# Segment attention with batch normalization: the last stage with groups in pairs in another order, two units each on ScalarE, rows by segment, nine buffers

## The chip, the cores and the metric

The kernel runs on one core of a Trainium2 chip. A core has TensorE (PE, matrix products into eight PSUM banks), VectorE (DVE), ScalarE (ACT), GpSimd (POOL, which here starts indirect DMAs) and SyncE (SP, which here starts plain DMAs). Each runs its own list of instructions in order, and they wait for one another by semaphores. The metric is the device time of one execution in microseconds (us).

## The reference

16,384 rows of 256 features carry a segment id from 0 to 7, and the ids are not sorted. A position is the row's index less the start that a binary search over the ids gives for its segment. Rows are put into a table of 8 segments by 3,072 positions (a negative position counts from the end, one beyond the table is dropped); each segment attends over itself, and each row reads its place in the result. A linear layer, a batch normalization over all rows, a ReLU and the residual follow:

```
starts = jnp.searchsorted(bids, jnp.arange(B, dtype=bids.dtype))
pos = jnp.arange(N, dtype=bids.dtype) - starts[bids]
...
scores = jnp.where(mask[:, None, :], scores, NEG)
attn = jax.nn.softmax(scores, axis=-1)
rp = jnp.einsum('blm,bmd->bld', attn, vp)
r = rp[bids, pos]
t = r @ Wt
mu = t.mean(axis=0)
var = t.var(axis=0)
tn = (t - mu) / jnp.sqrt(var + EPS) * gamma + beta
return feat + jax.nn.relu(tn)
```

## The kernel before

Only few rows have a place of their own in the table: at most six tiles of 128 rows per segment. All others read one of 16 edge rows (the first and last position of each segment). So there are two kinds of output.

**Segments (`for e in range(NB)`, lines 1581 to 1669).** For each segment the rows are gathered into `xs`, transposed, projected (`project`, `values`), and scored; `attend(e, u)` makes tile `u` on PE, and `attended(e, u)` takes DVE's reciprocal `rdens` and ACT's scaled copy into `tk`. Tiles 4 and 5 are present in some segments only (`present`, a branch on a register). `square` (ACT) and `moments` (DVE) add each tile and its square to `acc`, weighted by how many rows read it (`reads_r`). After tiles 3 and 5 `tk` is also stored to `t_rows` in HBM, from which POOL gathers the edge rows (`ecat`) and rows that are read twice (`tl`). In the last segment tiles 4 and 5 go through `attended` whether they are present or not, and the squares and sums of `tl` lie between its tiles.

**Sums (1671 to 1713).** PE adds the last segment's edge rows (`sel` by `tk`, into `b_e`), then the sums (`ones` by `acc`, `we` by `ecat`). DVE makes of these scale and shift (`ss`), and then the normalized edge rows in three bf16 parts, `y3`.

**Last stage (1723 to 1769).** The 16,384 output rows are 16 groups of 128 by 8 rows of 256, 1 MB each. Eight buffers `fb` hold groups: `group_in` loads one on SP. A group has four units of 2 rows (one PSUM bank each). A unit's one-hot matmuls (`hot`, 48 partitions, from partition 0 for groups 0 to 7 and from 64 for 8 to 15) pick the edge rows; three units are added to the loaded rows by DVE, one (`by_act`) gets the loaded rows through an identity matmul and is copied back by ACT. Then SP stores the group. After each group DVE normalizes three of the 48 tiles of `tk` (`normal`, three steps); the tiles of `tl` come after group 11.

These tiles must overwrite what the groups store, so POOL's row stores (`put`) of segment `e` wait until as many groups have landed as `upto[e]` says. SP counts these in `done` (`finish`), one group behind the store. The stores of `tl` wait for all 16:

```
1762        pg.op("POOL", lambda x, e=e: (x.wait_ge(done, 1), x.wait_ge(done, pg.regs[("POOL", ("g", e))])), [], [])
1767    pg.op("POOL", lambda x: x.wait_ge(done, NG), [], [])
```

**What sets the order.** A recorder (`Program.op`) notes every operation with the memory that it reads and writes, and derives the waits. Each engine executes its operations in the order of the text, so where a line stands in `fast_path` is where it stands in its engine's list. SP's list goes ahead of the others where it has nothing to wait for. `slot` puts pieces of table work into the segments' loop. At the end comes a check for inputs that this path can't handle (`bad`), and after a barrier a branch past the general path.

## Time and profile before

| | |
|---|---|
| median of three runs | 385.09 us (384.39 to 388.5) |
| profiled execution | 389.27 us, span of its records 387.2 us |
| busy in the span | PE 271.6, DVE 249.5, ACT 126.5, POOL 122.4 us |
| granted TensorE clock, mean | 0.795 |
| HBM traffic | 26.79 MB read, 28.74 MB written |
| last stage, from `y3` to the last row store | 273.9 to 370.8 us |

The helpers record all operations, so a line of the profile is a helper's line: L799 is a matmul, L818 a tensor-tensor operation, L809 an activation, L814 a copy on ACT, L874 a gather, L884 a row store, L869 a DMA on SP, L1750 a group's store, L1727 the count of `finish`. Operations are told apart by their tiles. `[0.84 <-DMA tl]` is idle time ahead of an operation and what ended it.

### The profile page before, as it was taken

To read this page: it belongs to the slowest core of one execution; us is meant where nothing else is said; L and a number is where in the kernel's file an instruction comes from. 1 tells how busy PE (TensorE), PEld (TensorE's weight loads), DVE (VectorE), ACT (ScalarE), POOL (GpSimd) and SP (SyncE) were. 2 spreads that over 40 slices of the span, in tenths; PEclk is the share of its full clock that TensorE was granted. 3 is DMA by queue.
4 is the path that set the end of the run, shared out by engine and by line. 5 is a ranking of instruction groups with operands and counts; after the bars stand their busy time and mean duration, and the time that the engine had idled before them with its cause. 6 is when DMAs were issued, how large, how long until landed. Compare 5 with 4: busy or idle time off the path is not lost.

```text
span 387.2 us, 4300 instructions
## 1 busy us (share of the span) xinstructions
PE 271.6 (70%) x1162; PEld 171.1 (44%) x1162; DVE 249.5 (64%) x728; ACT 126.5 (33%) x269; POOL 122.4 (32%) x120
## 2 busy tenths in 40 slices
PE   1247785892697899999999898854699999640000
PEld 1234463571374677677777685640243322110000
DVE  6674388697886767637638335365899999995000
ACT  0022522442434646835844736642011111010000
POOL 1623024061033015006006007620123377751720
PEclk9997788797888999999999999995555555555555
DMA  8971002121111213202202101259999999995200
GB/s 247 341 209 41 2 14 66 64 62 39 47 47 54 80 50 99 90 29 66 76 22 75 57 29 28 77 194 383 422 307 408 424 422 421 383 389 235 96 21 11
DMA packets 26000, 59.34 MB, mean 153 GB/s; under 512 B 5212, under 2 KB 18607, under 8 KB 21866
## 3 DMA queue, kind: packets, MB, share of 16 engines
q1 hardware_dynamic: 19242, 48.06, 33.1%
q0 software_dynamic: 5088, 10.19, 8.2%
q10 hardware_dynamic: 1632, 0.66, 0.6%
q8 instruction: 15, 0.25, 0.3%
q14 instruction: 23, 0.19, 0.2%
HBM read 26.79 MB, written 28.74 MB: 143 GB/s over the span
## 4 chain that ended last, share of the span: by engine, by line
PE 41%; DVE 26%; issue 10%; ACT 8%; DMA 6%; POOL 3%; SPq 1%; POOLq 0%; ACTq 0%; DVEq 0%
PE ps L799 39%; DMA out<-f 4%; DVE acc L838 3%; DVE f L818 3%; POOL out L884 3%; DVE tk L818 3%; ACT pb L809 2%; ACT tk L809 2%; DVE w L818 2%; DVE junk L825 2%; DVE k L815 2%; ACT pa L809 2%; PE ps L804 1%; DMA graw<-in_L_rec_beta 1%; ACT vs L814 1%
## 5 line engine op out<-in xcount | busy, mean ns | idle before, releaser
L874 POOL DMA_INDIRECT xs<-in_r_feat,idx x48 | 53.9, 1124 | 157.1 <-DVE idx L838 46.4
L799 PE MATMUL ps<-vs,pa 128*128 128x257 f32 x312 | 75.0, 388 | 1.8 <-ACT vs L814 1.8
L799 PEld LDWEIGHTS ps<-vs,pa 128*128 128x128 f32 x312 | 58.1, 192 | 15.4 <-issue 4.7
L884 POOL DMA_INDIRECT out<-tk,idx x39 | 44.0, 1128 | 40.0 <-SPq L1727 29.0
L809 ACT ACTIVATE tk<-ps,rdens 128x256 f32<-128x256 f32 x48 | 23.0, 479 | 79.1 <-DVE rdens L851 79.1
L799 PE MATMUL ps<-wvt,xT 128*128 128x256 f32 x156 | 43.1, 428 | 7.6 <-ACT vs L814 6.0
L799 PE MATMUL ps<-y,hot 48*128 48x256 bf16 x128 | 33.5, 409 | 12.8 <-DVE y L815 7.5
L799 PEld LDWEIGHTS ps<-wvt,xT 128*128 128x128 f32 x156 | 32.6, 215 | 20.9 <-ACT vs L814 7.7
L799 PEld LDWEIGHTS ps<-y,hot 48*128 48x128 bf16 x128 | 12.2, 123 | 51.6 <-issue 24.1
L799 PE MATMUL ps<-f,ident 128*128 128x512 f32 x32 | 33.2, 1140 | 0.0
L799 PE MATMUL ps<-q,k 32*128 32x512 f32 (+2 forms) x154 | 20.0, 530 | 16.0 <-ACT tk L809 16.0
L814 ACT COPY f<-ps 128x512 f32<-128x512 f32 x16 | 9.4, 585 | 66.6 <-PE ps L799 66.6
L818 DVE TENSOR_TENSOR tk<-tk,ss 128x768 f32<-128x768 f32 x32 | 30.5, 953 | 0.5
L818 DVE TENSOR_TENSOR f<-f,ps 128x512 f32<-128x512 f32 x48 | 30.0, 679 | 0.8 <-PE ps L799 0.8
L809 ACT ACTIVATE pa<-ps,mask 128x512 f32<-128x512 f32 x39 | 23.8, 687 | 18.2 <-PE ps L799 18.1
L838 DVE SCALAR_TENSOR_TENSOR acc<-tk,reads_r,acc 128x256 f32<-128x256 f32 x48 | 23.0, 479 | 10.5 <-ACT tk L809 10.3
L815 DVE COPY k<-ps 32x128 f32<-32x128 f32 x40 | 11.8, 294 | 24.2 <-PE ps L799 23.8
L838 DVE SCALAR_TENSOR_TENSOR acc<-sq,reads_r,acc 128x256 f32<-128x256 f32 x48 | 23.1, 481 | 1.8 <-ACT sq L809 1.8
L851 DVE RECIPROCAL rdens<-ps 128x1 f32<-128x1 f32 x48 | 7.8, 162 | 23.7 <-PE ps L799 23.4
L799 PE MATMUL ps<-xT,w 128*128 128x512 f32 (+1 forms) x60 | 22.6, 512 | 0.4 <-ACT xT L809 0.3
L799 PE MATMUL ps<-vs,pb 128*128 128x257 f32 x82 | 19.6, 387 | 0.0
L809 ACT ACTIVATE sq<-tk 128x256 f32<-128x256 f32 x48 | 19.2, 413 | 1.0
(231 smaller groups left out, 338.4 us busy)
## 6 DMA issues: line engine op xcount, KB each, us to landing
f<-in_r_feat SPq DMA_DIRECT2D x16, 1024.0 KB, 9.0
out<-f SPq DMA_DIRECT2D x16, 1024.0 KB, 9.9
xs<-zt SPq DMA_DIRECT2D x8, 768.0 KB, 10.2
t_rows<-tk SPq DMA_DIRECT2D x8, 512.0 KB, 2.9
t_rows<-tk SPq DMA_DIRECT2D x8, 256.0 KB, 2.2
eb<-edge_of SPq DMA_DIRECT2D x16, 96.0 KB, 2.4
xs<-in_r_feat,idx POOLq DMA_INDIRECT x48, 2.8
out<-tk,idx POOLq DMA_INDIRECT x39, 6.5
```

The costliest lines, as they stand in the source:

```text
L799: "PE", lambda e: e.matmul(out, lhsT, rhs, start=start, stop=stop, skip_group_check=True),
L804: return self.op("PE", lambda e: e.transpose(out, in_, ident), [in_, ident], [out])
L809: "ACT", lambda e: e.activation(out, in_, func, bias=bias, scale=scale), [in_, *more], [out]
L814: return self.op("ACT", lambda e: e.copy(out, in_), [in_], [out])
L815: return self.op(eng, lambda e: e.tensor_copy(out, in_), [in_], [out])
L818: return self.op(eng, lambda e: e.tensor_tensor(out, a, b, op), [a, b], [out])
L825: lambda e: e.tensor_scalar(out, a, s1, s2, op0, op1, accum_out=accum)
L838: else e.scalar_tensor_tensor(out, a, s, b, op0, op1),
L851: return self.op("DVE", lambda e: e.reciprocal(out, in_), [in_], [out])
L874: lambda e: e.indirect_dma_start(out=out, out_offset=None, in_=table, in_offset=bass.IndirectOffsetOnAxis(ap=ind, axis=0), bounds_check=n ...
L884: lambda e: e.indirect_dma_start(out=table, out_offset=bass.IndirectOffsetOnAxis(ap=ind, axis=0), in_=src, in_offset=None, bounds_check=n ...
```

## The change

- **Groups in pairs.** Groups are processed in an order of their own (`ORDER`: 0 to 6, 15 down to 12, 7 to 11), two at a time. The first of a pair uses one-hots on partitions 0 to 47, the second on 64 to 111, and their matmuls alternate. Two units of each group (`x >= 4`), not one, go through the identity matmul and ACT.
- **Gates.** `upto[e]` is now the highest turn among the groups that overlap a segment's positions, from both sides (`turn_of`).
- **Rows by segment.** After pair `c` DVE normalizes the rows of segment `c`: tiles 0 to 3 together, 4 and 5 each if present.
- **Buffers.** Nine instead of eight, over memory that is laid out anew. The first three loads are issued during segment 6, the others from segment 7 on as their memory comes free.
- **Sums.** The factor 1/N moves into `ones_n` and `we`. In the last segment the square of a tile is read from PSUM, tiles 4 and 5 are skipped if absent, the sums of tile 3 to 5 are made by PE (`by_reads`), and `tl` is gathered in segment 6, squared at once into `tq` ahead of the last segment's first tile, and added after its second. The edge rows gathered from `t_rows` are added by PE (`ident` by `ecat`).
- **Splitting `y3`** takes one operation less per part; `reads_r` of segment 6 is gathered; the check's DVE work moves to the first pair.

```diff
+    ORDER = (0, 1, 2, 3, 4, 5, 6, 15, 14, 13, 12, 7, 8, 9, 10, 11)
...
+        last = e == NB - 1
+        with present(e, u if last else 0):
+            pg.recip(rdens[:, m : m + 1], po[:, D : D + 1])
+        if last and u >= 4:
+            pg.set("DVE", spot2[:], 0.0)
+        with present(e, u if last else 0):
+            pg.act(tk[:, m, :], po[:, 0:D], AF.Identity, scale=rdens[:, m : m + 1])
+            if last:
+                pg.act(sq[m % 4][:], po[:, 0:D], AF.Square, scale=rdens[:, m : m + 1])
...
+            pg.tt(gcmp[:], gcmp[:], by_g(turn_of[:]), ALU.mult)
+            pg.red(grp[:], gcmp[:], ALU.max)
+            pg.ts(upto[:], grp[:], 1.0, ALU.max)
...
-    def group_in(g, after=()):
-        pg.dma("SP", fb[g][:], feat3[g], after)
+    def group_in(i, after=()):
+        pg.dma("SP", fb[i % NF][:], feat3[ORDER[i]], after)
...
+            if e >= NB - 3 and u == 2:
+                gather_reads(e + 1)
+            if e == NB - 2 and u == 3:
+                for t in range(LT):
+                    pg.gather(
+                        tl[:, t, :], t_rows[0 : (NB - 2) * FW, :], ridl[:, t : t + 1], (NB - 2) * FW
+                    )
+            if e == NB - 2 and u == 1:
+                group_in(0)
+            if e == NB - 2 and u == 4:
+                group_in(1)
+                group_in(2)
...
+    edges = pg.gather(ecat[:, 0, :], t_rows[0 : (NB - 1) * FW, :], eidx[:], (NB - 1) * FW)
+    pg.act(tq[:], tl[:], AF.Square)
+    for u in range(4):
+        attend(e, u)
+        for x in ready:
+            moments(*x)
+        ready = [(e, u)]
+        if u == 1:
+            for t in range(LT):
+                pg.tt(acc[:, 0, :], acc[:, 0, :], tl[:, t, :], ALU.add)
+                pg.tt(acc[:, 1, :], acc[:, 1, :], tq[:, t, :], ALU.add)
+        if u == 2:
+            for t in range(3, FT):
+                m = e * FT + t
+                pg.ts(by_reads[:, t - 3, :], ones_n[:], reads_r[:, m : m + 1], ALU.mult)
+        attended(e, u)
+        if u == 0:
+            group_in(3, [edges])
+        if u == 2:
+            scores(e, 1, None)
+            group_in(4)
+    group_in(5)
+    for u in (4, 5):
+        attend(e, u)
+        mark(ps_o[u % 2])
+        attended(e, u)
+    pg.mm(b_e[:, 0:D], ident[:], ecat[:, 0, :], start=True, stop=False)
+    pg.mm(sums[:], ones_n[:], acc[:].rearrange("p s d -> p (s d)"), start=True, stop=False)
...
+    for u in (4, 5, 3):
+        m = e * FT + u
+        with present(e, u):
+            pg.mm(sums[:, 0:D], by_reads[:, u - 3, :], tk[:, m, :], start=False, stop=False)
+            pg.mm(sums[:, D : 2 * D], by_reads[:, u - 3, :], sq[m % 4][:], start=False, stop=False)
+    for i in range(6, NF):
+        group_in(i)
...
-        pg.ts(yf[:], yh[:], later[:, s : s + 1], ALU.mult)
-        pg.tt(ye[:], ye[:], yf[:], ALU.subtract)
+        pg.stt(ye[:], yh[:], later[:, s : s + 1], ye[:], ALU.mult, ALU.add)
...
+    def rows(e):
+        m = e * FT
+        parts = [
+            ((lambda lo=lo: present(e, lo)), tk[:, m + lo : m + hi, :], xs[:, m + lo : m + hi, :], hi - lo)
+            for lo, hi in ((4, 5), (5, 6), (0, 4))
+        ]
+        normal(parts)
...
+    for c in range(NG // 2):
+        pair = (2 * c, 2 * c + 1)
+        for x in range(0, GT, 2):
+            by_act = x >= 4
+            pf = [bank[x + r] for r in range(2)]
             if by_act:
-                pg.mm(pf[:], ident[:], rows, start=True, stop=False)
+                for r, i in enumerate(pair):
+                    pg.mm(pf[r][:], ident[:], unit(i, x), start=True, stop=False)
             for u in range(2):
+                for r, i in enumerate(pair):
+                    h = slice(64 * r, 64 * r + 6 * NB)
+                    pg.mm(
+                        pf[r][:, u * D : (u + 1) * D], hot[h, c, x + u, :], y3[h, :],
+                        start=not by_act, stop=True,
+                    )
...
+            if i >= 2:
+                finish(stores[i - 2])
+                if i - 2 + NF < NG:
+                    group_in(i - 2 + NF)
+        rows(c)
```

Three places in the engines' lists, each before and after. The first is ACT at the passage from segment 6 to segment 7: `vs_66` are segment 7's values, the first `tk` below them is its tile 0, the names with `sq` are its square buffers, and `of_POOL_18` and the like are landings of gathers. Before:

```order
L814 COPY vs_66<-ps 128x2x256 [waits at_PE]
L809 ACTIVATE tk<-ps,rdens 128x256 [waits at_DVE]
L809 ACTIVATE sq_84<-tk 128x256 [waits at_ACT]
L809 ACTIVATE tk<-ps,rdens 128x256 [waits at_DVE]
L809 ACTIVATE sq_85<-tk 128x256 [waits at_ACT]
```

After:

```order
L814 COPY vs_66<-ps 128x2x256 [waits at_PE]
L809 ACTIVATE tq<-tl 128x768 [waits of_POOL_18,of_POOL_19,of_POOL_20]
L809 ACTIVATE tk<-ps,rdens 128x256 [waits at_DVE]
L809 ACTIVATE sq_72<-ps,rdens 128x256
L809 ACTIVATE tk<-ps,rdens 128x256 [waits at_DVE]
L809 ACTIVATE sq_73<-ps,rdens 128x256
```

The square of `tl` now stands ahead of tile 0, with a wait for three gathers.

The second is PE from the last segment's end to the sums; `ones,ident` is `mark`. Before:

```order
L799 MATMUL ps<-ones,ident 128x1 [waits at_ACT]
L799 MATMUL ps<-tk,sel 128x256 x3
L764 COMPARE_AND_BRANCH
L799 MATMUL ps<-tk,sel 128x256 [waits at_ACT]
L764 UNCONDITIONAL_BRANCH
L764 COMPARE_AND_BRANCH
L799 MATMUL ps<-tk,sel 128x256 [waits at_ACT]
L764 UNCONDITIONAL_BRANCH
L799 MATMUL ps<-tk,sel 128x256
L799 MATMUL ps<-acc,ones 128x512 [waits at_DVE]
L799 MATMUL ps<-ecat,we 128x512 [waits at_ACT]
```

After, up to the last `sel` (the `by_reads` products and `ecat,we` follow):

```order
L799 MATMUL ps<-ones,ident 128x1 [waits at_ACT]
L799 MATMUL ps<-ecat,ident 128x256 [waits of_POOL_21]
L799 MATMUL ps<-acc,ones_n 128x512
L799 MATMUL ps<-tk,sel 128x256 x3
L764 COMPARE_AND_BRANCH
L799 MATMUL ps<-tk,sel 128x256 [waits at_POOL,at_ACT]
L764 UNCONDITIONAL_BRANCH
L764 COMPARE_AND_BRANCH
L799 MATMUL ps<-tk,sel 128x256 [waits at_ACT]
L764 UNCONDITIONAL_BRANCH
L799 MATMUL ps<-tk,sel 128x256
```

The product with `acc` moved ahead of `sel`, `ecat,ident` is new, and so are the two to six products with `by_reads`.

The third is PE in the last stage; `y_99` and `y_102` are `y3`, the names with `f` the buffers. Before, one group:

```order
L799 MATMUL ps<-f_70,ident 128x512 [waits at_ACT,of_SP_14]
L799 MATMUL ps<-y_99,hot 128x256 x2
L799 MATMUL ps<-y_99,hot 128x256 [waits at_DVE]
L799 MATMUL ps<-y_99,hot 128x256
L799 MATMUL ps<-y_99,hot 128x256 [waits at_DVE]
L799 MATMUL ps<-y_99,hot 128x256
L799 MATMUL ps<-y_99,hot 128x256 [waits at_DVE]
L799 MATMUL ps<-y_99,hot 128x256
```

After, one pair:

```order
L799 MATMUL ps<-y_102,hot 128x256 [waits at_DVE] x2
L799 MATMUL ps<-y_102,hot 128x256 x2
L799 MATMUL ps<-y_102,hot 128x256 [waits at_DVE] x2
L799 MATMUL ps<-y_102,hot 128x256 x2
L799 MATMUL ps<-f_78,ident 128x512 [waits at_ACT,of_SP_13]
L799 MATMUL ps<-f_79,ident 128x512 [waits at_ACT,of_SP_15]
L799 MATMUL ps<-y_102,hot 128x256 x4
L799 MATMUL ps<-f_78,ident 128x512 [waits at_ACT]
L799 MATMUL ps<-f_79,ident 128x512 [waits at_ACT]
L799 MATMUL ps<-y_102,hot 128x256 x4
```

A pair has four identity products where two groups had two, and neighbouring one-hot products now belong to different groups.

More of the change, by code (lines that the diff above doesn't have):

```diff
@@ L988, in fast_path @@
     we = new("we", [2 * NB, P])
-    cnt_f = new("cnt_f", [P, NL])
+    cnt_f, turn_of = new("cnt_f", [P, NL]), new("turn_of", [1, NG])
     tmp_at = addr(tk) + (3 * FT - 2) * D * 4
@@ L1083, in fast_path @@
     pg.set("DVE", eps_t[:], EPS)
+    pg.set("DVE", ones_n[:], 1.0 / N)
+    pg.set("DVE", rdens[:], 1.0)
     def zero_fill(e):
@@ L1273, in attended @@
         m = e * FT + u
-        pg.recip(rdens[:, m : m + 1], po[:, D : D + 1])
-        pg.act(tk[:, m, :], po[:, 0:D], AF.Identity, scale=rdens[:, m : m + 1])
+        last = e == NB - 1
[7 more added lines that the diff above has]
+                pg.act(sq[m % 4][:], po[:, 0:D], AF.Square, scale=rdens[:, m : m + 1])
+        if last and u >= 4:
+            pg.copy("ACT", spot[:], ones[:, 0:1])
         if u in (3, 5):
@@ L1566, in fill_rows @@
     def fill_rows():
+        for i, g in enumerate(ORDER):
+            pg.set("POOL", turn_of[:, g : g + 1], float(i + 1))
         pg.set("DVE", xl[:], 0.0)
@@ L1580, in fast_path @@
     work.extend(everyone())
-    for e in range(NB):
+    for e in range(NB - 1):
         n = e + 1
-        if n < NB:
-            for eng in ("PE", "ACT", "DVE"):
-                pg.register(eng, n, tiles_i[0:1, n : n + 1], 2)
+        for eng in ("PE", "ACT", "DVE"):
+            pg.register(eng, n, tiles_i[0:1, n : n + 1], 2)
         if e == 0:
@@ L1613, in fast_path @@
             lag.append((e, u))
-            for _ in range(0 if e == 0 else 2 if u % 2 or e == NB - 1 else 1):
+            for _ in range(0 if e == 0 else 2 if u % 2 else 1):
                 if lag:
@@ L1686, in fast_path @@
-    sums = ps_s[1]
-    pg.mm(sums[:], ones[:], acc[:].rearrange("p s d -> p (s d)"), start=True, stop=False)
+    pg.act(ecat[:, 1, :], b_e[:, 0:D], AF.Square)
+    pg.copy("DVE", ecat[:, 0, :], b_e[:, 0:D])
     pg.mm(sums[:], we[:], ecat[0 : 2 * NB, :, :].rearrange("p s d -> p (s d)"), start=False, stop=True)
     pg.tr32(st_t[:], sums[:])
-    cols = st_t[:].rearrange("p (c i) -> p c i", i=32)[:, :, 0:1].rearrange("p c i -> p (c i)")
-    mqf = mq[:].rearrange("p s e -> p (s e)")
-    pg.ts(mqf, cols, 1.0 / N, ALU.mult)
+    mq = st_t[:].rearrange("p (s c i) -> p s c i", s=2, i=32)[:, :, :, 0:1].rearrange("p s c i -> p s (c i)")
@@ new lines, in fast_path @@
+            for r, i in enumerate(pair):
+                if by_act:
+                    pg.copy("ACT", unit(i, x), pf[r][:])
+                else:
+                    pg.tt(unit(i, x), unit(i, x), pf[r][:], ALU.add)
+        for i in pair:
+            f = fb[i % NF]
+            stores.append(
+                pg.op("SP", lambda e, i=i, f=f: e.dma_start(out3[ORDER[i]], f[:]), [f[:]], [], dma=True)
+            )
+            if i >= 2:
+                finish(stores[i - 2])
+                if i - 2 + NF < NG:
+                    group_in(i - 2 + NF)
```

192 lines of the change are left out of this document (75 added, 117 removed).

## The prediction

> **What bounds the kernel now.** I read the windows first: they show which stage runs on which limit.
>
> ```profile
> 240.00:250.00 10.00, 7.41 (x35) 5.28 (x36) 3.48 (x11) 6.24 (x13) 6.30 (x7) 1.00 0.25 81
> 270.00:280.00 10.00, 6.01 (x17) 2.73 (x18) 8.81 (x18) 0.58 (x1) 1.07 (x1) 0.50 1.00 403
> 300.00:310.00 10.00, 10.00 (x30) 3.46 (x30) 9.76 (x13) 1.76 (x3) 3.88 (x5) 0.50 1.01 422
> ```
>
> Columns: stretch, length, busy time of PE, PE weight loads, DVE, ACT, POOL, then granted clock, DMA share, GB/s. In the last stage DVE is full (9.76 of 10), the DMA engines are full too (share 1.01, 422 GB/s), and TensorE has half its clock; before 250 the DMA share is 0.25. The order of time for DVE, PE and SP shows the pitch:
>
> ```profile
> 273.63 0.29 DVE L815 CAST y<-ye 128x256 bf16<-128x256 f32 x1
> 278.72 4.16 SPq L1750 DMA_DIRECT2D out<-f  x2
> 279.19 2.07 PE L799 MATMUL ps<-f,ident 128*128 128x512 f32 x2
> 281.20 1.88 PE L799 MATMUL ps<-y,hot 48*128 48x256 bf16 x8
> 283.01 2.07 PE L799 MATMUL ps<-f,ident 128*128 128x512 f32 x2
> 293.29 1.87 DVE L818 TENSOR_TENSOR f<-f,ps 128x512 f32<-128x512 f32 x3
> 297.93 1.87 DVE L818 TENSOR_TENSOR f<-f,ps 128x512 f32<-128x512 f32 x3
> 351.91 0.96 DVE L838 SCALAR_TENSOR_TENSOR tk<-tk,xs 128x768 f32<-128x768 f32 x1
> ```
>
> `y3`, which everything in the last stage needs, is ready at 273.9. A group costs DVE 297.93 − 293.29 = 4.64 us; 16 groups are 74.2, and with the tl rows (2.9) DVE ends at 352.9. PE would need 283.01 − 279.19 = 3.82 per group. Then the end, on POOL:
>
> ```profile
> 295.67 1.25 POOL L884 DMA_INDIRECT out<-tk,idx  x1 [12.70 <-SPq L1727]
> 306.73 1.54 POOL L884 DMA_INDIRECT out<-tk,idx  x1 [5.19 <-SPq L1727]
> 344.84 0.99 POOL L884 DMA_INDIRECT out<-tk,idx  x1 [0.30 <-issue]
> 356.97 0.98 POOL L884 DMA_INDIRECT out<-tk,idx  x1 [11.14 <-SPq L1727]
> 369.86 0.98 POOL L884 DMA_INDIRECT out<-tl,idx  x1 [0.31 <-issue]
> ```
>
> After 31 row stores POOL waits 11.14 us for the last group, then issues the last 8 tk stores and 3 tl stores, (369.86 − 356.97) / 10 = 1.29 apart, to 370.84. That is 96.9 after `y3`; the remaining 16.4 to 387.2 hold no compute, and I leave them as they are.
>
> **The change: the tail.** The seeded ids give segment starts 0, 1441, 1441, 3121, 3677, 3677, 15838, 15838. With ±3072 positions, segments 0 to 5 touch groups 0 to 6 only, 6 and 7 only 12 to 15. ORDER processes just these first, so the gates become 3, 5, 5, 7, 7, 7, 11, 11 instead of "16" for the last two. Their 8 stores move ahead of the last group: 8 × 1.29 = 10.3 us off the end, if POOL keeps up.
>
> **DVE.** 32 PSUM sums instead of 48 at 1.87 / 3 = 0.62: 20.0. From the page's groups (count, busy us, mean ns), and from the rows by tile (min/median/max ns):
>
> ```profile
> L884 POOL DMA_INDIRECT out<-tk,idx x39 | 44.0, 1128 | 40.0 <-SPq L1727 29.0
> L818 DVE TENSOR_TENSOR tk<-tk,ss 128x768 f32<-128x768 f32 x32 | 30.5, 953 | 0.5
> ```
>
> ```profile
> L818 DVE TENSOR_TENSOR ye<-ecat,ss x1: 424/424/424, 270.0 to 270.0; 128x256 f32<-128x256 f32 x1
> L818 DVE TENSOR_TENSOR tl<-tl,ss x2: 944/952/959, 331.0 to 332.0; 128x768 f32<-128x768 f32 x2
> ```
>
> (953 − 424) / 512 is 1.03 ns per element, so a four-tile step is 1.22; 24 of them 29.3. The 39 row stores mean 7 single tiles beyond four per segment: 21 steps of 0.42, 8.9. Three tl steps 2.9. 48 conditional blocks are new to this place: between nothing and the 0.30 of the issue gaps on POOL, I take 0.12, 6 (0 to 14). Sum 67 (61 to 75), so DVE stops being last; what is late next is PE or DMA.
>
> **PE.** A pair has four identity units (2.01 each, 279.19 to 281.20) and 16 one-hot matmuls (8 take 1.81). If the two halves overlap, 16 cost about 1.1 × 8's time: 8.04 + 2.0 = 10.0 at half clock, 80 for eight pairs; 5.0 at full clock. Overlap of row groups is in the trace:
>
> ```profile
> 234.31 1.98 PE L799 MATMUL ps<-xT,w 128*128 128x512 f32 x4 [0.33 <-ACT xT L809]
> 240.74 1.14 PE L799 MATMUL ps<-q,k 32*128 32x512 f32 x8 [0.96 <-ACT tk L809]
> ```
>
> Eight 32-row matmuls on four row groups take 1.14, where eight of that width one after another would take 3.96. So the clock decides:
>
> ```profile
> 95.53:98.95 3.42, 3.34 (x11) 0.50 0.45 153
> 100.00:102.00 2.00, 2.00 (x8) 1.00 0.04 12
> 119.43:122.84 3.41, 3.41 (x7) 0.50 0.32 95
> 124.00:126.00 2.00, 2.00 (x17) 1.00 0.00 0
> 262.90:266.30 3.40, 3.40 (x4) 0.50 1.03 434
> 290.00:293.40 3.40, 3.40 (x10) 0.50 0.98 352
> ```
>
> Columns here: stretch, length, PE busy, clock, DMA. Two 3.4 us stretches filled with matmuls that use all 128 rows (or four 32-row groups at once) were followed by full clock. Two equally busy ones were not: in one half the time (264.44 on) went to a 16-row matmul, in the other (the last stage) 1.8 of every 3.8 us to 48-row one-hots. So I read the gate as following how much of the array works, not whether PE is busy. After the change 8 of 10 us are 128-row identity matmuls and the one-hots use 96 rows; I expect full clock within one or two windows of `y3`. By the Trainium skill ("TensorE: Matmul & The Clock Gate", Part 1) about 3.4 us of sustained activity is enough to release the clock; by that alone the stage before would have had full clock from 278, and it has 0.50 to the end, so the rows decide. By the page the first two rivals below would have no chance; the sum would stay.
>
> **DMA.** From the first store on: 16 stores and 7 loads (nine buffers are filled ahead) of 1.049 MB, 39 row stores of 0.131: 29.2 MB at 422 GB/s, 69.3 us (73 at 400). The first pair's stores need the whole pair: 8.7 after `y3` with the clock rising on the way (4.8 before). 8.7 + 69.3 + about 2 for issue and landing: last store at `y3` + 80.
>
> **POOL.** Puts between 306.73 and 344.84 come 38.11 / 26 = 1.47 apart. Store 4 (gate 5) is behind 7 MB: 8.7 + 17.5 + 3 = `y3` + 29.5; 35 puts later it is `y3` + 81, then 1 us for the last gate and 3 × 1.29: the last tl store ends at `y3` + 86. POOL and DMA are nearly level; either way it is 96.9 − 86 = 10.9 less than now.
>
> **When `y3` is ready.** This goes the other way.
>
> ```profile
> 105.89 3.61 PE L799 MATMUL ps<-wvt,xT 128*128 128x256 f32 x8 [3.52 <-ACT vs L814]
> 232.07 1.01 POOL L874 DMA_INDIRECT xl<-in_r_feat,idx  x1 [18.70 <-DVE idx L838]
> 246.82 1.00 POOL L874 DMA_INDIRECT reads_r<-reads_of,idx  x1 [0.30 <-issue]
> 249.80 0.47 ACT L809 ACTIVATE tk<-ps,rdens 128x256 f32<-128x256 f32 x1 [1.53 <-DVE rdens L851]
> 250.31 0.42 ACT L809 ACTIVATE sq<-tk 128x256 f32<-128x256 f32 x1
> 251.29 0.99 POOL L874 DMA_INDIRECT tl<-t_rows,ridl  x1 [0.30 <-issue]
> 254.09 0.42 DVE L818 TENSOR_TENSOR acc<-acc,tl 128x256 f32<-128x256 f32 x1 [0.84 <-DMA tl<-t_rows,ridl]
> 262.06 0.48 DVE L838 SCALAR_TENSOR_TENSOR acc<-sq,reads_r,acc 128x256 f32<-128x256 f32 x1
> 262.59 1.92 PE L799 MATMUL ps<-acc,ones 128*128 128x512 f32 x2 [3.94 <-DVE acc L838]
> 264.44 2.07 PE L799 MATMUL ps<-ecat,we 16*128 16x512 f32 x2
> 266.55 0.72 DVE L854 STREAM_TRANSPOSE st_t<-ps 128x512 f32<-128x512 f32 x1 [3.68 <-PE ps L799]
> 271.61 0.35 DVE L827 TENSOR_SCALAR yf<-yh,later 128x256 f32<-128x256 bf16 x1
> ```
>
> The new square `tq` stands on ACT ahead of `tk` of the last segment's first tile, and waits for three tl gathers. POOL is busy with reads_r to 247.8, so the gathers start at 248.1, 249.4, 250.7; landing takes 254.09 − 251.29 = 2.8: 253.5. `tq` is three times as wide as the 0.42 square, about 0.8 with one start-up for three, so that `tk` starts at 254.3 instead of 249.80. Queued behind it on ACT are all tiles of segment 7; DVE and PE wait for those. Then six tl sums (2.5) stand before the second reciprocal. Counting tile by tile (0.2 reciprocal, 0.5 tk, 0.5 square, 0.45 per moment; 0.6 for by_reads), the last square ends at 263.7, although tiles 4 and 5 are now skipped: 262.54 was DVE's end before. From there PE does ecat, acc, four sel, by_reads and we: 14 f32 instructions of 256 columns and 4 of 512. At half clock these take 3.61 / 8 = 0.45 and 1.92 / 2 = 0.96, together 10.1; at full clock (1.98 / 4 = 0.50 for 512, half that for 256) 5.5. With the square and copy of ecat between: 6 to 11, against 3.96 now. I take 7.8, since the tile before it is dense 128-row work: st_t at 271.5 (269.7 to 275). The scale `mq` (0.2) and, twice, the product `yf` (0.35) go: `y3` at 278, 4 later than now (2 to 7.5). The early loads I cost at nothing: three come before 250, where the DMA share was 0.25, and nine at 2.5 each fit before 276. On SP, loads 1 and 2 stand ahead of the t_rows store of segment 6's last tiles, which the edge gather waits for; they start near 240.7, when that segment's fourth tile is done, and are through by 246.5, before that store is ready at 247. If not, up to 2.5 more. The six added reads_r gathers (7.8) lie in POOL's 18.7 us gap before 232.07.
>
> **Sum.** 278 + 86 + 16.3 = 380.3 against a span of 387.2: −6.9. The profiled execution took 389.27 (2.1 outside the span), the median of the runs is 385.09; the difference off the median gives 378.
>
> **Rivals.** *Half clock to the end.* For it: 24 us of full PE at 0.50 in the last stage. Against: the mix changes from half to four fifths dense rows. Then PE sets the pace at 10.0 per pair: 80 + 0.6 + 8 for the last two stores in a row is `y3` + 89; POOL, gated later, ends about `y3` + 96: 390.3, +3.1, 388 on the median. Within 1% or just over.
> *Slower: halves that do not overlap.* If the 48-row pairs run in turn, and the clock stays low, a pair costs 8.04 + 3.62 = 11.7, with the waits between pieces 12; eight make 93 to 96, the last stores land at `y3` + 102, the end is `y3` + 107: 401, or 399 on the median. Eight pitches and 11 more reach today's 92.8 after `y3` at 278 (370.8) with a pitch of 10.2: from there on it decides; the four-group rows above speak against it.
> *`y3` not later.* If the gathers land by 250, `tq` hides and the sums run at full clock: `y3` at 274.5, 374.5 on the median. Against: POOL's reads end at 247.8.
> *The gates don't fall* (the segments need the last group after all): then 8 stores come back to the end, +10.3, level with before. The starts above exclude it for these ids.
>
> **Numbers.** Forecast 0.62, its own range 374 to 383 (`y3` 276 to 281, DMA at 400 or 422 GB/s). Half clock 0.20, no overlap 0.08, earlier `y3` 0.08, anything else 0.02 and slower. About 1% is what a measurement of this kernel can tell from no change. Faster: 0.55 of the forecast plus 0.08; same: 0.07 plus 0.13 of half clock; slower: 0.07, 0.08 and 0.02. The range that holds four of five is 372 to 389.
>
> **What would show it.** Right: the last two gates of POOL open before the last store, with only three tl stores behind it; granted clock 1.00 for part of each pair; DVE under 80% in the last stage; DMA share 1.0 until the last store; an ACT wait on `tl` before the first tile of segment 7, and `y3` near 278. Wrong: clock 0.50 throughout with a pair pitch of 10 us or more; one-hots of a pair taking 3.6 at half clock; `y3` at 274; or an idle POOL while DMA is far from full.

## The result: 374.6 us, and the profile after

The changed kernel takes 374.6 us (median of four runs, 374.13 to 376.37) beside 385.7 for the kernel before (four runs, 384.39 to 388.5): a ratio of 0.971, 95% interval 0.965 to 0.978. It is faster, by 2.9%; 378 was predicted, with 374 to 383 as the forecast's own range. The profiled execution took 374.63 us, its span is 372.9, and the mean granted TensorE clock rose from 0.795 to 0.871.

The windows of the changed kernel, in the columns of the table before (PE, PE weight loads, DVE, ACT, POOL, clock, DMA share, GB/s):

```profile
270.00:280.00 10.00, 7.95 (x33) 3.18 (x34) 8.77 (x18) 1.68 (x4) 0.52 (x1) 0.66 0.25 100
280.00:290.00 10.00, 10.00 (x49) 3.98 (x49) 9.90 (x14) 4.47 (x9) 0.00 (x0) 1.00 0.93 350
320.00:330.00 10.00, 4.86 (x19) 1.94 (x19) 4.76 (x6) 1.91 (x4) 7.87 (x8) 0.84 1.01 416
340.00:350.00 10.00, 0.00 (x0) 0.00 (x0) 0.00 (x0) 0.00 (x0) 7.56 (x9) 0.50 0.96 375
```

DVE is as full as before from 280 to 320 (9.8 to 9.9 of every 10 us), but from 320 to 330, where it was busy 9.7 of 10 before, half of its time is free. The clock is 1.00 at 280 where it was 0.50. DMA is nearly full from the first store on (0.93 to 1.02 up to 350), and of the engines POOL alone works at the end. The hole is new: between the last load and the first store, 273 to 280, the DMA engines move nothing. In order of time:

```profile
271.70 0.29 DVE L815 CAST y<-ye 128x256 bf16<-128x256 f32 x1
280.05 5.26 SPq L1807 DMA_DIRECT2D out<-f  x3
291.16 1.02 POOL L884 DMA_INDIRECT out<-tk,idx  x1 [20.64 <-SPq L1778]
303.64 0.98 POOL L884 DMA_INDIRECT out<-tk,idx  x1 [7.18 <-SPq L1778]
337.92 0.98 POOL L884 DMA_INDIRECT out<-tk,idx  x1 [0.31 <-issue]
353.38 0.99 POOL L884 DMA_INDIRECT out<-tk,idx  x1 [0.30 <-issue]
357.26 0.98 POOL L884 DMA_INDIRECT out<-tl,idx  x1 [0.31 <-issue]
```

`y3` is ready at 272.0. Gate 5 opens at 303.64; from there POOL issues 35 row stores and the three of `tl` without a wait, (353.38 − 303.64) / 34 = 1.46 apart, to 358.24. Even the count of all 16 groups, which the stores of `tl` wait for, costs nothing any more: POOL is the later one. The groups of the page:

```profile
L884 POOL DMA_INDIRECT out<-tk,idx x39 | 44.7, 1147 | 39.1 <-SPq L1778 27.8
L818 DVE TENSOR_TENSOR f<-f,ps 128x512 f32<-128x512 f32 x32 | 19.9, 682 | 6.1 <-DMA f<-in_r_feat 5.2
L799 PE MATMUL ps<-f,ident 128*128 128x512 f32 x64 | 39.7, 746 | 9.1 <-DMA f<-in_r_feat 9.1
L799 PE MATMUL ps<-y,hot 48*128 48x256 bf16 x128 | 13.1, 291 | 10.3 <-DVE y L815 6.6
```

PE and DVE now wait for loads. The spans differ by 387.2 − 372.9 = 14.3. By parts: 2.6 had been gained by the first reciprocal of segment 0 (51.67 against 54.23); from there to `y3` it takes 220.3 instead of 219.7 (0.6 lost); from `y3` to POOL's last store 86.2 instead of 96.9 (10.7 gained); what follows 14.7 instead of 16.4 (1.7 gained, in a stretch where no engine is busy).

### The profile page after: what moved, and what is told of

Same layout as the page of the kernel before. It is cut to its first block, busy times and chain, and to the rows that moved or that the text cites. A ratio compares the mean times of both kernels' runs of the same rounds, so it can differ in the third digit from the quotient of the medians.

```text
span 372.9 us, 4444 instructions
## 1 busy us (share of the span) xinstructions
PE 258.7 (69%) x1200; PEld 171.2 (46%) x1200; DVE 228.5 (61%) x707; ACT 132.3 (35%) x281; POOL 129.9 (35%) x143
## 4 chain that ended last, share of the span: by engine, by line
PE 37%; DVE 22%; DMA 16%; ACT 8%; issue 6%; POOL 4%; SPq 1%; POOLq 0%; ACTq 0%; DVEq 0%
PE ps L799 36%; DMA out<-f 13%; DVE acc L838 3%; POOL out L884 3%; ACT pb L809 2%; DVE w L818 2%; ACT tk L809 2%; DVE junk L825 2%; DVE k L815 2%; PE ps L804 1%; SPq L869 1%; DMA graw<-in_L_rec_beta 1%; ACT pa L809 1%; DMA t_rows<-tk 1%; ACT vs L814 1%
## 5 line engine op out<-in xcount | busy, mean ns | idle before, releaser
L799 PE MATMUL ps<-vs,pa 128*128 128x257 f32 x312 | 77.2, 395 | 5.1 <-ACT sq L809 3.2
L799 PEld LDWEIGHTS ps<-vs,pa 128*128 128x128 f32 x312 | 59.6, 197 | 19.0 <-ACT sq L809 4.0
L799 PE MATMUL ps<-f,ident 128*128 128x512 f32 x64 | 39.7, 746 | 9.1 <-DMA f<-in_r_feat 9.1
L814 ACT COPY f<-ps 128x512 f32<-128x512 f32 x32 | 17.2, 589 | 52.4 <-PE ps L799 52.4
L799 PE MATMUL ps<-q,k 32*128 32x512 f32 (+2 forms) x154 | 19.2, 505 | 16.0 <-ACT tk L809 16.0
L818 DVE TENSOR_TENSOR tk<-tk,ss 128x1024 f32<-128x1024 f32 (+1 forms) x30 | 24.3, 849 | 0.3
L818 DVE TENSOR_TENSOR f<-f,ps 128x512 f32<-128x512 f32 x32 | 19.9, 682 | 6.1 <-DMA f<-in_r_feat 5.2
L799 PEld LDWEIGHTS ps<-f,ident 128*128 128x128 f32 x64 | 12.6, 224 | 23.7 <-DMA f<-in_r_feat 12.2
L851 DVE RECIPROCAL rdens<-ps 128x1 f32<-128x1 f32 x46 | 7.5, 162 | 24.6 <-PE ps L799 24.4
L799 PE MATMUL ps<-xT,w 128*128 128x512 f32 (+1 forms) x60 | 20.6, 477 | 0.4 <-ACT xT L809 0.3
L799 PE MATMUL ps<-y,hot 48*128 48x256 bf16 x128 | 13.1, 291 | 10.3 <-DVE y L815 6.6
L799 PEld LDWEIGHTS ps<-y,hot 48*128 48x128 bf16 x128 | 5.1, 97 | 29.3 <-issue 15.5
```

The costliest lines, as they stand in the source:

```text
L799: "PE", lambda e: e.matmul(out, lhsT, rhs, start=start, stop=stop, skip_group_check=True),
L814: return self.op("ACT", lambda e: e.copy(out, in_), [in_], [out])
L818: return self.op(eng, lambda e: e.tensor_tensor(out, a, b, op), [a, b], [out])
L851: return self.op("DVE", lambda e: e.reciprocal(out, in_), [in_], [out])
```

## The experiments

Runs of one group ran on the same chip; each ratio is to runs of the kernel before on that chip, whose median was 387.1 (A), 393.6 (B), 386.5 (C) and 392.0 (D). The two columns at the right are from each run's profile, in us.

| group, run | median us | ratio, 95% interval | first reciprocal to `y3` | `y3` to POOL's last store |
|---|---|---|---|---|
| before | 385.7 | 1 | 219.7 | 96.9 |
| changed | 374.6 | 0.971 (0.965 to 0.978) | 220.3 | 86.2 |
| A before again | 388.6 | one run | 219.8 | 96.6 |
| A natural order | 383.4 | 0.988 (0.984 to 0.992) | 221.6 | 93.8 |
| A halves not side by side | 378.2 | 0.978 (0.971 to 0.984) | 221.6 | 87.5 |
| A one unit on ACT | 373.2 | 0.964 (0.959 to 0.969) | 217.7 | 84.9 |
| B `tq` later | 390.3 | 0.995 (0.991 to 0.998) | 235.9 | 86.7 |
| B no early loads | 392.8 | 0.999 (0.996 to 1.002) | 238.8 | 85.0 |
| B later loads | 392.3 | 0.994 (0.989 to 0.999) | 239.1 | 86.2 |
| B first stores in halves | 393.5 | 0.999 (0.995 to 1.004) | 239.0 | 86.7 |
| C changed again | 375.7 | 0.973 (0.961 to 0.986) | 220.6 | 85.5 |
| C early `tl` undone | 382.7 | 0.989 (0.979 to 0.999) | 226.7 | 86.6 |
| C that, with three edits | 381.6 | 0.988 (0.982 to 0.994) | 225.7 | 85.8 |
| D `tq` later, one unit | 382.8 | 0.978 (0.972 to 0.984) | 228.5 | 85.4 |

**Is the lead at segment 0 the change's?** The kernel before, unchanged.

> The kernel before once more, unchanged, for a second profile. In the first profile y3 was ready at 273.9 and the first reciprocal of segment 0 stood at 54.23; in the profile of the changed kernel they stand at 272.0 and 51.67. Theory: the 2.5 us by which the changed kernel leads at segment 0 belong to the execution (granted clock 0.85 and 0.81 between 20 and 60 us, against 0.91 and 0.91), so this profile may show a first reciprocal anywhere from 51 to 55, and y3 at about that + 219.7 again (first profile: 273.9 - 54.2). Rival: the change itself makes the early segments faster (nothing in the diff does work there except on POOL); then the first reciprocal is at 54.2 again, within 0.5.

The first reciprocal is at 54.01, so this run alone speaks for the rival. But the runs made from the changed kernel, which are alike up to there, have it anywhere from 49.78 to 53.96. The lead of 2.6 lies within what executions differ by; two profiles of the kernel before don't settle whether the change has a share in it. From here on the time from there to `y3` is compared, with care: it is 219.7 and 219.8 in the kernel before, but five profiles of code that is alike up to `y3` (changed, changed again, natural order, halves apart, one unit) have anything from 217.7 to 221.6. Steadier is the time from the first reciprocal of segment 7: 24.3 in both profiles of the kernel before, 24.4 to 24.9 in these five.

**What is the order of the groups worth?**

```diff
-    ORDER = (0, 1, 2, 3, 4, 5, 6, 15, 14, 13, 12, 7, 8, 9, 10, 11)
+    ORDER = tuple(range(16))
```

> The changed kernel with the groups in their natural order, 0 to 15, all else as changed; the gates of segments 6 and 7 then need the last store again. Theory (POOL, with 39 + 3 puts, has become the bound, so part of what the order saves was given back): POOL still does 31 puts by about 343, waits for the last store, which lands near 348 since 8 puts are not yet in the way, and then issues 8 + 3 puts 1.29 apart: last put ends near 362.2 instead of 358.2. About 4 us more than the changed kernel's 374.6: 378.6, ratio to the kernel before 0.981. Rival (the step of the prediction taken alone: 8 puts of 1.29 return in full): +10.3, 385, ratio 0.998. Rival (the order saves nothing): 374.6, 0.971.

POOL's order of time in this run; `y3` was at 275.6:

```profile
355.49 0.98 POOL L884 DMA_INDIRECT out<-tk,idx  x1 [8.81 <-SPq L1778]
368.39 0.98 POOL L884 DMA_INDIRECT out<-tl,idx  x1 [0.30 <-issue]
```

The last gate opens 79.9 after `y3`, and eight tk and three tl stores follow. The end is 7.6 later after `y3` than in the changed kernel (93.8 − 86.2; 8.3 against its second profile): between the two expectations, 4 and 10.3, since the last group lands 79.9 after `y3` and not 76, as I had reckoned here. Of the 10.3 that the order takes from the end, the rest is given back, because POOL's 42 stores, pitched at 1.46, now end last.

**Do the halves overlap, and what sets the clock?** The two groups of a pair one after the other, with the same instructions.

```diff
-            for u in range(2):
-                for r, i in enumerate(pair):
+        for r, i in enumerate(pair):
+            for x in range(0, GT, 2):
...
+                for u in range(2):
```

> The changed kernel with the two groups of a pair issued one after the other, so that the one-hot matmuls of the two halves of TensorE no longer stand next to each other; same instructions, same stores. One-hots of a pair then take 16 x 0.235 = 3.8 us at half clock (1.88 for eight in the kernel before), identity units 8.04: 11.8 at half clock, 5.9 at full. Theory (the granted clock follows the share of the array's rows that work): in the kernel before the last stage had (2.0 x 128 + 1.8 x 48) / 3.8 = 90 rows on average and half clock; the changed kernel has about 121 and full clock; this one has (8.04 x 128 + 3.8 x 48) / 11.8 = 102, between the two. If that is enough for full clock, pairs of 5.9 stay under the transfers' pace and the time is 374.6 + 1 = 375.6, ratio 0.974, with granted clock 1.00 within 5 us of y3. If it is not, the pitch is 11.8, the last store is issued near y3 + 96 and the time is about 391, ratio 1.013: the slower rival of the prediction. Rival theory (busy time alone sets the clock): full clock, 0.974.

PE in order of time, first of the changed kernel:

```profile
284.64 1.99 PE L799 MATMUL ps<-f,ident 128*128 128x512 f32 x4
286.56 0.39 PE L799 MATMUL ps<-y,hot 48*128 48x256 bf16 x4
286.88 1.99 PE L799 MATMUL ps<-f,ident 128*128 128x512 f32 x4
288.80 0.83 PE L799 MATMUL ps<-y,hot 48*128 48x256 bf16 x12
289.56 1.99 PE L799 MATMUL ps<-f,ident 128*128 128x512 f32 x4
```

and of this run:

```profile
285.48 0.61 PE L799 MATMUL ps<-y,hot 48*128 48x256 bf16 x6
286.03 1.13 PE L799 MATMUL ps<-f,ident 128*128 128x512 f32 x2
287.08 0.39 PE L799 MATMUL ps<-y,hot 48*128 48x256 bf16 x2
287.40 1.12 PE L799 MATMUL ps<-f,ident 128*128 128x512 f32 x2
288.46 0.61 PE L799 MATMUL ps<-y,hot 48*128 48x256 bf16 x6
```

A pair takes 289.56 − 284.64 = 4.92 with overlap (5.0 predicted) and 2 × (288.46 − 285.48) = 5.96 without (5.9 expected). The overlap is real and worth 1 us per pair, but here hardly any of the time: 0.978 against 0.971, intervals that overlap, since from the third pair on DVE sets the pace: from its first sum of that pair to the first of the seventh it takes 31.7 us in the changed kernel and 31.6 here, 7.9 per pair. The slower rival needed the low clock as well, and that did not come. The windows show when the clock rises, first in the changed kernel (`y3` at 272.0):

```profile
275.05:276.05 1.00, 1.00 (x3) 0.17 (x1) 1.00 (x2) 0.00 (x0) 0.00 (x0) 0.50 0.00 0
276.05:277.05 1.00, 1.00 (x5) 0.11 (x4) 0.97 (x2) 0.00 (x0) 0.00 (x0) 0.67 0.00 0
277.05:278.05 1.00, 1.00 (x5) 0.52 (x4) 0.96 (x2) 0.84 (x2) 0.00 (x0) 1.00 0.00 0
```

then in this run (`y3` at 273.0):

```profile
280.02:281.02 1.00, 1.00 (x2) 0.00 (x0) 1.00 (x2) 0.00 (x0) 0.00 (x0) 0.67 0.50 197
281.02:282.02 1.00, 1.00 (x5) 0.41 (x4) 0.97 (x2) 0.41 (x1) 0.00 (x0) 1.00 1.05 434
```

**Are two units on ACT needed?**

```diff
-            by_act = x >= 4
+            by_act = x >= 6
```

> The changed kernel with one unit of each group on ScalarE instead of two: 48 PSUM sums on VectorE instead of 32, two identity matmuls less per pair. Theory: 16 x 0.62 = 9.9 us more on VectorE, whose work after y3 becomes 67 + 10 = 77 us; the pitch of the first pairs is VectorE's (6 x 0.62 + about 4.2 for the rows = 7.9 instead of 5.0), so store 4 and with it gate 5 come 0 to 4 us later, and the end by as much: 375 to 379, ratio 0.973 to 0.983. Rows working on TensorE are (4.02 x 128 + 2.06 x 96) / 6.08 = 117 while it works, so the clock should reach 1.00 within 5 us of y3. Rival: the second unit on ScalarE is what raises the clock; then the granted clock stays at 0.50 through the first pairs, as before (VectorE would hide it, since 6.1 us per pair is under 7.9).

The windows of this run (`y3` at 271.5):

```profile
274.58:275.58 1.00, 1.00 (x2) 0.34 (x1) 1.00 (x3) 0.00 (x0) 0.00 (x0) 0.50 0.07 29
275.58:276.58 1.00, 1.00 (x10) 0.33 (x10) 1.00 (x2) 0.00 (x0) 0.00 (x0) 0.95 0.07 29
```

The rival fell, and of the theory the time: it is not longer but 373.2, the same as the changed kernel's within the intervals. DVE is full to the end again (9.8 to 9.9 of 10 from 280 to 340), yet the end comes 84.9 after `y3`: while the clock is still low the first pair has two identity products less on PE, its stores are issued at 277.35 (`y3` + 5.8 instead of 8.0), and that seems to pay for the slower pairs behind it; gate 5 at least, which was to open up to 4 us later, opens at `y3` + 29.7 instead of 31.6. What held of the theory is the clock, which is full after 4 us with one unit too. The change's second unit on ScalarE buys nothing that can be measured.

Together these runs narrow down what raised the clock. One unit without overlap (before, about 90 rows at work on average) stays at 0.50 to the end, although PE has no gap in its work from 274 to 312; two units without overlap (102), one unit with (117) and two with (121) reach 1.00. Either edit suffices; no run takes back both and keeps the rest of the change. The averages are over whole pairs; in the changed kernel the rise itself, at 276.7, comes in the first pair's identity products, which use all 128 rows:

```profile
273.02 3.78 PE L799 MATMUL ps<-f,ident 128*128 128x512 f32 x4
```

Busy time alone doesn't decide: in the run with `tq` later (below) PE works 2.82 of the 3.41 us from 254.27 to 257.68, all of it with 128-row matmuls, and the clock is 1.00 right after, while PE without a gap stayed at 0.50 in the kernel before. That the rows decide fits all of this; another measure of the work that orders the cases alike is not excluded.

**What does the wait for `tl` cost?**

```diff
-    pg.act(tq[:], tl[:], AF.Square)
     for u in range(4):
...
+        if u == 2:
+            pg.act(tq[:], tl[:], AF.Square)
```

The six sums on `acc` move behind the loop over the four tiles.

> The changed kernel with the square tq moved on ScalarE from ahead of segment 7's first tile to after its second, and the six tl sums on VectorE moved behind the reciprocal of its fourth tile; same work, only later in each engine's order. Theory (the prediction's term for y3, with the size that the profile of the changed kernel gives): there the reciprocal of the first tile is at 247.46 and its tk, behind tq, at 249.95, so 2.3 us of wait go, and 2.0 us of sums leave the way between the first and the second reciprocal: y3 up to 4 us earlier, 370.6, ratio to the kernel before 0.961. Rival (the edge gather, which lands near 251, and PE's sums set y3): y3 within 1 us of where it was, ratio 0.971.

`y3` is 3.0 earlier than in the other three runs of its group (235.9 against 238.8 to 239.1), and the median 2 to 3 us lower. But it isn't the wait that went. The whole group came 18 us late to `y3`, by stops that are told of below, and so `tl` had landed in good time. ACT and DVE of the run with later loads (below), of the same group, in which `tq` stands early:

```profile
265.98 0.85 ACT L809 ACTIVATE tq<-tl 128x768 f32<-128x768 f32 x1
268.27 0.17 DVE L851 RECIPROCAL rdens<-ps 128x1 f32<-128x1 f32 x1 [3.68 <-PE ps L799]
```

`tq` has no wait there and is done before the first reciprocal. What moving it saved are the six sums (1.7 us from the first reciprocal to the second, instead of 3.6), and 1.2 us on PE between the last square and `st_t` (6.2 instead of 7.4), where the clock was 1.00 throughout in this run and 0.50 for 3.4 us in the others. The wait itself, 2.3 us, is seen in the changed kernel's own rows, in the part on the prediction.

**Did the early loads cost or bring anything?** Loads 0 to 2 back behind the edge gather.

> The changed kernel with the three loads of feat that stand inside segment 6 moved back behind the edge gather in segment 7. Theory (they cost nothing and bring nothing up to the first store, as the prediction has it): nine loads of 2.5 us from 251.6 on, with the rows between, are in by 276, and the first pair is ready only at 280; the time stays at 374.6, ratio 0.971. Rival 1 (they delayed the row stores that the edge gather waits for): y3 up to 2.5 earlier without them, ratio 0.965. Rival 2 (loads now run into the sums and the first store): up to 2.5 later, 0.977.

Nothing that shows here: 238.8 to `y3`, beside 239.0 and 239.1, and 0.999 beside 0.994 and 0.999. But in this group the stops left the loads time to pass. In the first profile of the changed kernel the edge gather starts 5.4 us after the `t_rows` store that it waits for was issued (243.45 to 248.83), 2.9 in the kernel before, with the DMA engines full of loads when it was issued (share 0.95): the loads do hold that store up. It costs nothing there, since the way to `y3` goes through `tl`, whose gathers stand ahead of the edge gather.

**POOL or the transfers?** Loads two stores later.

```diff
-                if i - 2 + NF < NG:
-                    group_in(i - 2 + NF)
+            if i >= 4 and i - 4 + NF < NG:
+                group_in(i - 4 + NF)
```

> The changed kernel with each later load of feat issued two stores later (after store i the load of group i+5 instead of i+7); the counting of landed stores stays where it was. Theory (POOL is the bound from gate 5 on, and that gate waits for store 4, which stands behind loads in the DMA queues): stores 0 to 4 then follow each other, store 4 lands near 295 instead of 303.6, POOL's 35 puts behind it end near 346, and the end passes to the transfers: the last store still lands near 350, three puts behind it end at 354 instead of 358.2. About 4 less than the changed kernel: 370.6, ratio 0.961. Rival (the transfers are the bound already): the same time, 0.971. Rival (late loads starve the pairs): the DMA engines run dry near 300 and the time grows by 2 to 5, ratio 0.976 to 0.984.

POOL, `y3` at 290.5:

```profile
309.48 1.02 POOL L884 DMA_INDIRECT out<-tk,idx  x1 [20.42 <-SPq L1778]
373.14 0.98 POOL L884 DMA_INDIRECT out<-tl,idx  x1 [4.78 <-SPq L1778]
```

The mechanism came as told: gate 5 no longer stops POOL, which is through 4.78 before the last group lands. That group lands only at `y3` + 82.6, and the end is where it was, `y3` + 86.2. In time the first rival holds, though not by its reason, since in the changed kernel POOL did not wait for the last group: transfers and POOL end within a few us of each other, and relieving one brings up the other.

**The hole ahead of the first store.** Halves of the first pair's groups stored as soon as they are summed.

```diff
+            if c == 0 and x == 2:
+                for i in pair:
+                    half.append(group_out(i, 0, 4))
```

> The changed kernel with the first pair's stores split in two halves of half a megabyte, the first halves issued as soon as four of a group's eight rows per partition are summed. In the changed kernel the DMA engines stand idle from 273 to 280, between the last load and the first store. Theory (the start of the stores sets the transfers, and through store 4 the gates): first bytes leave at y3 + 4.5 instead of y3 + 8.0, all later landings move by about 3, the end too: 371.6, ratio 0.963. Rival (gate 5 hangs on the pace of VectorE and TensorE in pairs 1 and 2, not on the queue): 374.6, 0.971. The run with one unit on ScalarE fits the theory: there pair 0 was stored at y3 + 5.8 instead of 8.0 and the ratio was 0.964.

The first bytes leave 2.7 after `y3` (292.98), but the second pair is stored no earlier, the DMA share sinks to 0.75 at 300 to 310 instead, and gate 5 opens at `y3` + 32.0 (31.6 in the changed kernel). The rival holds: the hole only moves.

**The changed kernel again, and the early `tl` sums undone.** In the second run the reads of segment 6 come from the test against its length again (six gathers less), the `tl` gathers stand behind the edge gather, `tq` and the sums behind the last tile.

> The changed kernel once more, unchanged, beside the two runs below on the same chip. In the last four runs, all made from the changed kernel and run together, PE, VectorE and ScalarE stood still together twice, near 212 to 220 and between 249 and 262, while GpSimd issued the reads_r gathers of segment 6 and of segment 7; y3 came 239 us after the first reciprocal instead of 220. In the first profile of the changed kernel, and in the three runs before those four, there is no such stop. Theory A (the stops belong to the place where those four ran, since the same gathers ran without a stop elsewhere): this run shows y3 about 220 after the first reciprocal and a ratio of 0.971 if it runs elsewhere, 239 and 0.995 to 1.000 if it runs there. Theory B (one of the four edits caused them): impossible for all four alike unless this run is free of stops in the same place.

> The changed kernel with its early tl sums undone: segment 6 takes its read counts from the test against its length again, so the six added reads_r gathers of GpSimd go, and the three tl gathers stand behind the edge gather as before; the square tq and the six sums stand behind segment 7's last tile, and the matmul of acc behind the four with sel. Theory 1 (the prediction's term: the added gathers cost nothing, but tq ahead of segment 7's first tile costs 2.3 and the sums 2.0): y3 2 to 4 earlier than in the changed kernel, 371 to 372.5, ratio 0.962 to 0.966, where there are no stops. Theory 2 (the added gathers also stop the other engines where the stops occur): there the first stop, of about 8, goes with them and only the one of segment 7's own gathers stays; 10 to 12 less than the changed kernel in the same place. Rival (tl now lands late, near 255, and acc with it): y3 within 1 us, ratio 0.971.

The changed kernel gives 0.973 and 220.6: its result stands. Undoing the early sums makes `y3` 6.1 later (226.7) and the time 7 us longer; neither theory nor the rival had that. Up to the last square theory 1 is right: from segment 7's first reciprocal to the end of that square it takes 6.5 us, beside 10.9 in the changed kernel on the same chip, which is 4.4 less where 2.3 and 2.0 were counted. But then ACT waits for `tl`. POOL and ACT of that run:

```profile
257.51 1.00 POOL L874 DMA_INDIRECT tl<-t_rows,ridl  x1 [0.30 <-issue]
265.42 0.84 ACT L809 ACTIVATE tq<-tl 128x768 f32<-128x768 f32 x1 [9.14 <-DMA tl<-t_rows,ridl]
```

The last gather lands 6.9 us after its issue ends; in the changed kernel it is 249.20 − 248.08 = 1.1. Behind the edge gather it stands in the DMA queues among the loads of `feat` that the edge gather had let go (DMA share 1.00 from 260 to 270). And the edge gather ahead of it starts only at 253.50, after 5.8 us of waiting for a `t_rows` store. That is what the move to segment 6 saves. My edit did not hold the loads back until `tl` was in, as the kernel before does, so it does not price the move against the kernel before.

**Two attempts at a faster kernel.** First the kernel just told of, with later loads, halves, and one unit on ACT in the first pair; then, in D, the changed kernel with `tq` later and one unit throughout.

> The kernel of the run above (early tl sums undone) with three edits more: loads of feat two stores later, the first pair with one unit on ScalarE instead of two, and the first pair's stores in halves. Theory: after y3 the transfers are the bound (with late loads alone the last store landed at y3 + 82.5 while GpSimd had its rows out at y3 + 77.8), so only an earlier first store counts; it leaves at about y3 + 3.5 instead of 8.0 and the second pair 2 us earlier, so the last store lands at about y3 + 80 and the end comes 2 to 3 earlier than in the run above: 369 to 370, ratio 0.956 to 0.959, where there are no stops. Rival (GpSimd is the bound through its 42 stores): no gain over the run above.

> The changed kernel with two edits that did not hurt before: tq and its sums later (it took 2.5 us off beside its neighbours, where the engines stopped twice), and one unit on ScalarE instead of two (y3 + 84.9 at the last row store instead of y3 + 86.2). Theory (the wait of ScalarE for tl is on the way to y3 without those stops too, and the first pair is short with two identity matmuls less at half clock): y3 about 3 earlier after the first reciprocal, 217 to 218, the last row store at y3 + 85: 370 to 371, ratio 0.957. Rival (both were within what the measurement can tell): 0.964 to 0.973, no difference from the changed kernel.

Neither beats the changed kernel where it was measured: 0.988, no gain over 0.989 for the kernel it is built on, and 0.978, where the stops (below) are back. From `y3` on they take 85.8 and 85.4. One of the ten executions of the first took 852.42 us, for which nothing on record gives a reason. Whether the second is faster where there are no stops wasn't tried; from segment 7's first reciprocal to `y3` it takes 19.2 us, and the run with `tq` later 19.5, against 24.4 to 24.9 in the changed kernel without stops, so that by an estimate from these some 4 us may be left there.

## Why the prediction was right, and where it was off

- **After `y3`: right, by its own numbers.** POOL's last store was forecast at `y3` + 86 and came at 86.2: pitch 1.47 forecast, 1.46 measured; gate 5 at 29.5 forecast, 31.6 measured; first store at 8.7, came at 8.0; the last group's landing at 80, which the run in natural order shows at 79.9. POOL as the bound, with DMA nearly level, is what the runs with later loads and with halves bear out.
- **The gates: right,** with only three stores behind the last count. Of the 10.3 us taken from the end 7.6 stay.
- **DVE: right that it stops being the last.** One row of the windows holds its work after `y3`:

```profile
272.05:340.00 67.95, 51.01 (x194) 18.03 (x194) 58.69 (x86) 17.18 (x32) 33.73 (x28) 0.83 0.89 358
```

  58.7 us, done by 337.92. The forecast of 67 counted 6 for the conditional blocks. Of these next to nothing is seen: DVE is idle for 6.6 us up to then, and all but 0.6 of it are waits for a load (5.2) or for PE (0.9). The rest is 2 less than forecast. What was not seen is that up to 320 DVE still sets the pace of the pairs, and that it didn't have to be relieved so far: one unit gives the same time.
- **Clock and overlap: right.** A pair of 4.92 where 5.0 was forecast, clock full 4.7 us after `y3` (0.67 on average in the second from 276.05 puts the step at 276.7). By the Trainium skill ("TensorE: Matmul & The Clock Gate", Part 1) about 3.4 us of sustained activity release the clock; the rise in the changed kernel, at 4.7, would agree; the one at 7.7 with the halves apart and PE busy throughout, and the 38 us without a gap at 0.50 in the kernel before, do not. The two rivals fall with the clock: half clock to the end did not occur in any run.
- **When `y3` is ready: the term that was mis-sized.** 4 us later was forecast (2 to 7.5); measured from the first reciprocal it is 0.6, and from that of segment 7 0.1 to 0.6. The wait itself was there, in the order of time of the changed kernel:

```profile
247.09 0.99 POOL L874 DMA_INDIRECT tl<-t_rows,ridl  x1 [0.30 <-issue]
247.46 0.17 DVE L851 RECIPROCAL rdens<-ps 128x1 f32<-128x1 f32 x1 [3.05 <-PE ps L799]
249.20 0.84 ACT L809 ACTIVATE tq<-tl 128x768 f32<-128x768 f32 x1 [3.30 <-DMA tl<-t_rows,ridl]
249.95 0.46 ACT L809 ACTIVATE tk<-ps,rdens 128x256 f32<-128x256 f32 x1
257.61 0.47 ACT L809 ACTIVATE sq<-ps,rdens 128x256 f32<-128x256 f32 x1
265.48 0.72 DVE L854 STREAM_TRANSPOSE st_t<-ps 128x512 f32<-128x512 f32 x1 [1.21 <-PE ps L799]
```

  `tk` of the first tile starts 2.3 after its reciprocal (4.5 forecast), because the gathers landed at 249.2 and not at 253.5: they took 2.1 from the start of the last one, not 2.8, and POOL's list was further ahead, 2.6 of it from the start of the execution. The tiles behind it follow in a somewhat shorter row than my sum of pieces, which laid reciprocal, copy, square and moments end to end where engines overlap: 8.1 us from that `tk` to the end of the last square, not 9.4. So this square ends at 258.1, not 263.7, of which 2.6 again are the execution's lead. The sums by PE were sized rightly: 265.48 − 258.08 = 7.4, with 7.8 taken. So the rival "`y3` not later" (374.5) came nearest in time, though not by its mechanism: `tq` did not hide, and the sums ran at half clock for part of their time.
- **The end: 1.7 less than assumed,** 14.7 instead of 16.4 behind the last row store, and 14.4 to 14.7 in the other profiles made from the changed kernel, except in the two with the early `tl` sums undone, which have 16.2. The DVE part of the test for unusual inputs left that stretch, but in these two it is gone from there as well, so that this is not the cause; what is stays open.
- **Early loads at nothing: nothing on record against it,** though they do hold up the store that the edge gather waits for. The added `reads_r` gathers at nothing: right where the result was measured, and perhaps dear elsewhere, as the last section tells.

Together: −6.9 forecast on the profiled execution, less 3.4 for `y3` and 1.6 for the end, makes −11.9; the spans, without the 2.6 of the lead, differ by 11.7, the medians by 11.1.

## What to carry to other kernels

When several limits end within a few us of each other, as POOL and the transfers do here, size each to the last landing before pricing an edit: what one gives up, the next takes back (7.6 of 10.3 stayed; later loads and halved stores, each with its mechanism at work, gave nothing). A small gather that a chain waits for belongs ahead of the bulk loads in the queues, not only ahead of its reader: the run that put it behind them, with other edits that by themselves took 4.4 us off, came 6 us later to `y3`. And a sum of instruction times along a tile's chain is an upper bound where the next tile's pieces run beside it.
